# Expert outputs scattered to rows of their tokens, and w2 read in place by TensorE, in a retention and mixture-of-experts kernel

## The chip, the cores and the metric

The kernel runs on one core of a Trainium2 chip. The metric is the device time of one execution in microseconds (us), lower is better. Everything is float32.

## What is computed

Two sequences of 4096 tokens with 256 features each pass through one layer: a retention block with a gate, a layer norm, a mixture of eight experts of which each token uses two, and a second layer norm. Cut to what matters:

```python
q, v  = x @ Wq.T, x @ Wv.T                    # 16 heads of 16
state[t] = lam * state[t-1] + v[t]            # per channel, along the sequence
y     = layernorm(q * state) * ln_g + ln_b
x1    = layernorm(x + (y * silu(x @ Wg.T)) @ Wo.T)
gates = softmax(x1 @ gate_W)                  # 8 experts
cw    = the two largest gates, divided by their sum; 0 elsewhere
out   = x1
for e in range(8):
    h   = relu(x1 @ W1[e] + b1[e])            # 256 -> 512
    out = out + cw[:, e:e+1] * (h @ W2[e] + b2[e])   # 512 -> 256
out   = layernorm(out)
```

## The kernel before

**Tiles.** The 8192 tokens are 16 blocks of TB = 512, each held as 128 partitions x NT = 4 rows. `attention(i)` is a generator that does one block up to the routing; its `yield`s cut it into steps, which the main loop interleaves with steps of the neighbouring blocks and with expert work.

**Routing.** Each block's tokens find their two experts on VectorE (`largest`), and a matmul with a triangle of ones (lines 451 and 452) gives each token its row in its expert's region of a DRAM buffer `xs`. Eight indirect DMAs from GpSimd (line 470), one for each of 4 x 2 sets of 128 rows, scatter the rows of `x1` there. The blocks form two groups (`GROUPS = (13, 3)`: blocks 0 to 12 and 13 to 15), each with its own `xs` and `ys` buffers in DRAM. `plan_slots` turns the counts into slots: 256 rows of one expert where an expert has filled so many (SL = 256), and after the last block of a group slots of 128 rows for what is left, padded with zero rows that GpSimd writes (`put_zeros`, line 205). Group 0 has 45 slots of 256 and 21 of 128, group 1 has 5 and 21. Tiles and lines of the slots of 128 carry `_rest` in the profile.

**A slot.** `load_slot` reads the slot's row and expert number into SyncE registers and loads its 256 or 128 rows (`xg`) and the expert's w1 from DRAM. `slot_columns` transposes the rows on TensorE (line 590), VectorE copies them out (line 591), ScalarE reads the expert's number into a register (line 592) and copies that expert's w2, b2 and b1, 1284 floats per partition, from a table `kept` of all eight experts to a tile `wb` (line 596). `slot_first` is h (TensorE line 608, ScalarE's relu line 615), `slot_second` is h @ w2 (TensorE line 629, weights `hT`, moving operand `wb`) and VectorE's addition of b2 (line 633, output `ysl`, two buffers). `store_slot` writes the rows with a DMA from SyncE to `ys`, to the same rows as they had in `xs` (line 638); each store waits for the store before it.

**Combining.** When the last slot of a group is stored, `to_gather` gets all its blocks. `gather` takes 128 tokens: two indirect DMAs from GpSimd (line 654) read the tokens' two rows from `ys` by the row numbers `pos`, and at the first of a block SyncE loads the block's `x1` back (line 650, tile `sum`, three buffers). `weigh` adds the two rows with their weights on VectorE (line 669) and takes the statistics (lines 675 and 676), three gathers later (AHEAD = 3). `scale_of` makes the second norm's factor (a power on GpSimd, line 238), `end` applies it on ScalarE (line 689) and stores the block.

**Order.** TensorE, VectorE, ScalarE and SyncE run their instructions in the order in which the program lists them (`manual_schedule`). GpSimd isn't in that list, so the framework's scheduler orders its queue by itself. `half` does one half of a slot, and with it some combining of the group that is finished, paced by `debt`, so that group 0 is combined while group 1's slots run. Group 1 is combined after the last slot.

Of the kernel before, what the change touches and what calls it, by code (L numbers as in the profile page):

```python
# [15 lines left out]
P = 128  # L16
TB = 512
# [3 lines left out]
AHEAD = 3  # L21
# [10 lines left out]
def kernel(  # L32
# [22 lines left out]

    nc = tc.nc
# [18 lines left out]
    KEPT = NF * D + D + NF  # L75
# [5 lines left out]
    lam_sb = const.tile([P, NC, TB], FP, tag="lam", name="lam_sb")  # L81
# [43 lines left out]
    kept = const.tile([P, E, KEPT], FP, tag="kept", name="kept")  # L125

    def keep(e, after):
        at = 0
        for src, n in (
            (w2[e].rearrange("(c p) d -> p c d", p=P), NF),  # L130
            (b2[e : e + 1].partition_broadcast(P), 1),
            (b1[:, ts(e, NF)].unsqueeze(1), 1),
        ):
            size = n * src.shape[-1]
            dma = nc.sync.dma_start(
                out=kept[:, e, at : at + size].rearrange("p (c f) -> p c f", c=n), in_=src
            )
            at += size
            if after is not None:
                tc.add_manual_dep(dma.ins, after, SYNC, reason="not all at once")  # L140
                after = None
# [14 lines left out]
    m_rows = const.tile([1, MAXS, E], FP, tag="m_rows", name="m_rows")  # L156
    nc.vector.tensor_scalar_mul(m_rows, m_tab, float(SL))

    zeros = const.tile([P, D], FP, tag="zeros", name="zeros")
    nc.gpsimd.memset(zeros, 0.0)  # L160

    class Group:


        def __init__(self, k, n_blocks):
            self.k, self.n_blocks = k, n_blocks
            self.full = max(0, 4 * n_blocks - 7)
            self.rest = 8 * n_blocks + 7 - 2 * self.full
            assert self.rest <= MAXS
            self.cap = n_blocks * TB + P  # L170
            self.dump = E * self.cap
            rows = self.dump + (E - 1) * P
            self.xs = dram.tile([rows, D], FP, tag=f"xs_{k}", name=f"xs_{k}")
            self.ys = dram.tile([rows, D], FP, tag=f"ys_{k}", name=f"ys_{k}")

            self.first = const.tile([P, E], FP, tag=f"first_{k}", name=f"first_{k}")
            nc.gpsimd.iota(self.first, [[self.cap, E]], base=0, channel_multiplier=0,
                           allow_small_or_imprecise_dtypes=True)
            self.base = self.first
            self.taken = const.tile([1, E], FP, tag=f"taken_{k}", name=f"taken_{k}")  # L180
            nc.vector.memset(self.taken, 0.0)
            self.filled = []
            self.stored = []

            self.dumps = const.tile([1, MAXS, E], FP, tag=f"dumps_{k}", name=f"dumps_{k}")
            nc.vector.tensor_scalar(
                self.dumps, m_tab, float(E - 1 - self.rest), 0.0, ALU.add, ALU.max
            )
            nc.vector.tensor_scalar(
                self.dumps, self.dumps, float(P), float(self.dump), ALU.mult, ALU.add  # L190
            )
            self.off = const.tile([1, MAXS, E], FP, tag=f"off_{k}", name=f"off_{k}")
            nc.vector.scalar_tensor_tensor(
                self.off, m_tab, float(P), self.dumps, ALU.mult, ALU.subtract
            )
# [8 lines left out]
        def put_zeros(self, row):  # L204
            self.put(nc.gpsimd.dma_start(
                out=self.xs[ds(row, P), :], in_=zeros
            ))
# [7 lines left out]
        def store(self, dma):  # L215
            key = f"ys_{self.k}"

            tc.declare_no_dep(
                dma.ins, group=key, keep=self.stored[-1:], reason="rows of their own"
            )  # L220
            tc.add_to_no_dep_group(key, dma.ins)
            self.stored.append(dma.ins)

    groups = [Group(k, n) for k, n in enumerate(GROUPS)]
    for m in range(E - 1):
        for gr in groups:
            gr.put_zeros(gr.dump + m * P)
# [45 lines left out]
    def project(w, xT, o, name):  # L273
# [13 lines left out]
        dram.tile([P, NT, D], FP, tag=f"x1_{i}", name=f"x1d_{i}") for i in range(NB)  # L287
# [3 lines left out]
    def attention(i):  # L291
# [7 lines left out]
        for o in range(NC):  # L299
            v_ps = project(wv_sb, xT, o, f"v_{i}_{o}")  # L300
            first = i % BPS == 0
            nc.vector.tensor_tensor_scan(  # L302
                state[:, o, :],
                lam_sb[:, o, :],
                v_ps,
                0.0 if first else states[i - 1][:, o, TB - 1 : TB],
                ALU.mult,
                ALU.add,
            )
# [48 lines left out]
        rr = work.tile([P, NT, D], FP, tag="x1", name=f"x1_{i}", bufs=3)  # L358
        for t2 in range(NT // 2):
            o_ps = ps_a.tile([P, 2, D], FP, tag="pa", name=f"ao_{i}_{t2}")  # L360
            for u in range(2):
# [6 lines left out]
                rr[:, 2 * t2 : 2 * t2 + 2, :], o_ps, x_t[:, 2 * t2 : 2 * t2 + 2, :], ALU.add  # L368
# [3 lines left out]
        mv = row_stats(lambda t: rr[:, t, :], f"a{i}")  # L372
        r = rstd_of(mv[:, :, 1:2], f"a{i}")
        yield
        normalise(x1, lambda t: rr[:, t, :], mv, r, f"a{i}")
# [35 lines left out]
        def largest(src, name, hot):  # L411
# [9 lines left out]
            return top  # L421

        hot = small.tile([P, 2, NT, E], FP, tag="hot", name=f"hot_{i}")
        top1 = largest(g, "1", hot[:, 0])
# [3 lines left out]
        top2 = largest(rest, "2", hot[:, 1])  # L428
# [50 lines left out]
    def schedule(gr, j):  # L479
# [3 lines left out]
        if j == gr.n_blocks - 1:  # L483
# [3 lines left out]
            for e in range(E):  # L487
                gr.put_zeros(
                    nc.values_load(
                        ends[:, e : e + 1], engines=[ENG.Pool],  # L490
                        min_val=e * gr.cap, max_val=(e + 1) * gr.cap - P,
                    )
                )
            plan_slots(gr, f"{gr.k}_rest", gr.rest, True)

    def plan_slots(gr, name, n, rest):
# [52 lines left out]
        if rest:  # L549
            nc.vector.tensor_tensor(plan[:, 0, :n, :], at, gr.dumps[:, :n, 0:1], ALU.add)  # L550
        else:
            nc.vector.tensor_copy(plan[:, 0, :n, :], at)
# [7 lines left out]
    def load_slot(s):  # L560
# [8 lines left out]
        xg = slot.tile([P, SL // P, D], FP, tag="xg", name=f"xg_{name}", bufs=3)  # L569
# [13 lines left out]
    def slot_columns(s):  # L583
# [7 lines left out]
        nc.vector.tensor_copy(xgT, pt)  # L591
        e = nc.values_load(
# [4 lines left out]
        return gr, name, size, row, xgT, w1_t, wb[:, 0, :]  # L597

    def slot_first(s):
        gr, name, size, row, xgT, w1_t, wb = s  # L600
        b1_t = wb[:, NF * D + D :]
# [16 lines left out]
        return gr, name, size, row, hT, wb  # L618

    def slot_second(s):  # L620
        gr, name, size, row, hT, wb = s
        n_t = size // P
        w2_t = wb[:, : NF * D].rearrange("p (c d) -> p c d", c=NF)
        b2_t = wb[:, NF * D : NF * D + D].unsqueeze(1)
        y = slot.tile([P, SL // P, D], FP, tag="ysl", name=f"ysl_{name}")[:, :n_t, :]
        po = ps_s.tile([P, SL // P, D], FP, tag="ps", name=f"po_{name}")[:, :n_t, :]
        for t in range(n_t):
            for f in range(NF):
                nc.tensor.matmul(  # L629
                    po[:, t, :], hT[:, f, ts(t, P)], w2_t[:, f, :],  # L630
# [3 lines left out]
        return gr, size, row, y  # L634

    def store_slot(s):
        gr, size, row, y = s
        gr.store(nc.sync.dma_start(
            out=gr.ys[ds(row, size), :].rearrange("(p t) d -> p t d", p=P), in_=y
        ))  # L640
        left[gr.k] -= size // P
        if left[gr.k] == 0:
            to_gather.extend((i, t) for i in place if place[i][0] is gr for t in range(NT))

    def gather(i, t):

        gr, _ = place[i]
        if t == 0:
            sums[i] = work.tile([P, NT, D], FP, tag="sum", name=f"sum_{i}", bufs=3)
            nc.sync.dma_start(out=sums[i], in_=x1_dram[i])  # L650
        both = []
        for k in range(2):
            yk = work.tile([P, D], FP, tag=f"y{k}", name=f"y{k}_{i}_{t}", bufs=AHEAD + 2)
            dma = nc.gpsimd.indirect_dma_start(  # L654
                out=yk.bitcast(I32),
                out_offset=None,
                in_=gr.ys.bitcast(I32),
                in_offset=bass.IndirectOffsetOnAxis(ap=poss[i][:, k, t, :], axis=0),
            )
            for ins in gr.stored:  # L660
                tc.add_manual_dep(dma.ins, ins.name, SYNC, reason="rows stored before")
            both.append(yk)
        return i, t, both

    def weigh(i, t, both):

        x1, wt = sums[i], wts[i]
        for k, yk in enumerate(both):
            nc.vector.scalar_tensor_tensor(  # L669
                x1[:, t, :], yk, wt[:, k, t, :], x1[:, t, :], ALU.mult, ALU.add  # L670
# [4 lines left out]
        nc.vector.bn_stats(st, x1[:, t, :])  # L675
# [8 lines left out]
    def end(i):  # L684
# [3 lines left out]
        for t in range(NT):  # L688
            nc.scalar.activation(
                x1[:, t, :], x1[:, t, :], AF.Identity,  # L690
                bias=less[:, t, :], scale=r[:, t, :],
            )
        nc.scalar.dma_start(out=ob[i], in_=x1)

    loaded, turned, hidden, out_of = [], [], [], []
    to_gather, gathered, to_scale, to_end = [], [], [], []
# [13 lines left out]
    def combining():  # L710
        return to_gather or gathered or to_scale or to_end

    def some_combining(n):

        for _ in range(n):
# [4 lines left out]
            if to_gather:  # L720
                gathered.append(gather(*to_gather.pop(0)))
            if len(gathered) > AHEAD or (gathered and not to_gather):
                weigh(*gathered.pop(0))

    def half():
# [17 lines left out]
        debt[0] += len(to_gather) * size / (P * max(1, 2 * sum(left.values()) - 8))  # L743
# [14 lines left out]
    lam_col = const.tile([P, NC], FP, tag="lam_col", name="lam_col")  # L758
    nc.vector.tensor_copy(lam_col, lam_ps[:, :NC])
    for c in range(NC):  # L760
        nc.vector.tensor_copy(lam_sb[:, c, :], lam_col[:, c : c + 1].broadcast_to([P, TB]))
# [87 lines left out]
```

## Time and profile before

| | |
|---|---|
| median of 3 runs | 1097.53 us (1095.64 to 1101.23) |
| the profiled execution's own time | 1091.48 us |
| its span, first to last instruction | 1089.5 us |
| TensorE, VectorE, ScalarE, GpSimd busy | 899.7, 548.4, 386.1, 318.5 us |
| granted TensorE clock, mean | 0.924 |
| moved by DMA | 163.79 MB |

How to read it: PE is TensorE's matmuls, PEld its weight loads, DVE is VectorE, ACT ScalarE, POOL GpSimd, SP SyncE; a q behind an engine means its sequencer, which handles registers, waits and the issue of DMAs. A group of instructions is shown as line, engine, operation, output <- inputs, count, busy time in us and mean ns of one, then the engine's idle time before them and what ended it. In a table by stages each engine's column is its busy time in that stretch, with the number of instructions. "DMA share" is the mean busy share of the 16 DMA engines.

### The profile page before, as it was taken

Reading aid. Unit: us, or ns where it says so; the run is one execution under the profiler, and the core shown is the slowest. Engines: PE = TensorE matmul, PEld = TensorE weight load, DVE = VectorE, ACT = ScalarE, POOL = GpSimd, SP = SyncE. Lnnn points to the kernel's source line nnn. Section 1 sums busy time; section 2 is a strip of 40 time slices with the busy share of each in tenths; the row PEclk is TensorE's granted clock in tenths of the full one; section 3 lists DMA queues with packets and bytes.
Section 4 is the critical chain, followed back from the end, with each engine's and each line's share of the span. In section 5 each row is a group of like instructions: output and inputs, shape, how many; then the busy total and the mean of one; then the engine's idle time right before and its main releaser. Section 6 shows DMA issues by size and latency. Waiting matters only on the chain. (4 is left out here: it accounts for less than half of the span.)

```text
span 1089.5 us, 14838 instructions
## 1 busy us (share of the span) xinstructions
PE 899.7 (83%) x4366; PEld 713.7 (66%) x4366; DVE 548.4 (50%) x1841; ACT 386.1 (35%) x733; POOL 318.5 (29%) x346
## 2 busy tenths in 40 slices
PE   4988586899899999999999999999898965776710
PEld 2555354778677777778786868688797854666610
DVE  2675544356455554555455455534334245665544
ACT  1221212323333334343333323334454423554412
POOL 3112321302030303030211203130304367676454
PEclk9998796999999999999999999999899988888965
DMA  5611214232333424242434342443647857988653
GB/s 192 205 54 44 88 60 143 99 124 88 133 119 126 151 101 161 94 151 88 146 102 131 112 131 97 164 155 128 193 155 226 269 182 246 281 296 267 229 175 110
DMA packets 95041, 163.79 MB, mean 150 GB/s; under 512 B 12081, under 2 KB 45361, under 8 KB 94961
## 3 DMA queue, kind: packets, MB, share of 16 engines
q1 hardware_dynamic: 68800, 107.52, 30.6%
q0 software_dynamic: 13728, 37.50, 10.4%
q10 hardware_dynamic: 12432, 17.84, 4.5%
q8 instruction: 34, 0.56, 0.2%
q14 instruction: 47, 0.38, 0.1%
HBM read 106.72 MB, written 56.10 MB: 149 GB/s over the span
## 5 line engine op out<-in xcount | busy, mean ns | idle before, releaser
L629 PE MATMUL po<-wb,hT 128*128 128x256 f32 x800 | 190.3, 393 | 8.1 <-issue 6.2
L608 PE MATMUL ph<-xgT,w 128*128 128x256 f32 x800 | 185.8, 386 | 10.4 <-DVE xgT L591 10.4
L608 PEld LDWEIGHTS ph<-xgT,w 128*128 128x128 f32 x800 | 154.1, 194 | 36.9 <-DVE xgT L591 11.2
L629 PEld LDWEIGHTS po<-wb,hT 128*128 128x128 f32 x800 | 153.6, 197 | 29.7 <-issue 7.1
L470 POOL DMA_INDIRECT xs<-x,pos x128 | 124.4, 972 | 142.8 <-DVE rows L512 102.1
L615 ACT ACTIVATE hT<-ph,wb 128x256 f32<-128x256 f32 x200 | 83.9, 471 | 211.3 <-PE ph L608 149.8
L654 POOL DMA_INDIRECT y<-ys,pos x128 | 125.5, 981 | 81.3 <-issue 29.9
L238 POOL TENSOR_TENSOR rstd_a<-rstd_a,half_neg 128x4 f32<-128x4 f32 x16 | 16.1, 1007 | 429.5 <-DVE rstd_a L237 429.5
L629 PE MATMUL po_rest<-wb_rest,hT_rest 128*128 128x256 f32 x336 | 89.6, 415 | 18.0 <-DVE rstd_f L237 12.8
L608 PE MATMUL ph_rest<-xgT_rest,w_rest 128*128 128x128 f32 x672 | 89.3, 290 | 18.2 <-DVE xgT_rest L591 12.4
L591 DVE COPY xgT<-xt 128x512 f32<-128x512 f32 x50 | 34.5, 691 | 137.1 <-PE xt L590 110.1
L608 PEld LDWEIGHTS ph_rest<-xgT_rest,w_rest 128*128 128x128 f32 x672 | 86.9, 204 | 24.1 <-DVE xgT_rest L591 14.2
L615 ACT ACTIVATE hT_rest<-ph_rest,wb_rest 128x128 f32<-128x128 f32 x168 | 48.1, 369 | 116.3 <-PE ph_rest L608 45.8
L629 PEld LDWEIGHTS po_rest<-wb_rest,hT_rest 128*128 128x128 f32 x336 | 67.0, 210 | 29.1 <-issue 16.3
L633 DVE TENSOR_TENSOR ysl<-po,wb 128x512 f32<-128x512 f32 x50 | 34.3, 686 | 85.9 <-PE po L629 33.5
L276 PE MATMUL g<-xT,wg_sb 128*128 128x512 f32 x128 | 61.4, 621 | 8.4 <-DVE state L302 5.0
L596 ACT COPY wb<-kept 128x1284 f32 x50 | 63.1, 1262 | 3.8 <-DVE ysl L633 0.9
L669 DVE SCALAR_TENSOR_TENSOR sum<-y,wt,sum 128x256 f32<-128x256 f32 x128 | 61.5, 481 | 5.5 <-DMA y<-ys,pos 3.3
L276 PE MATMUL q<-xT,wq_sb 128*128 128x512 f32 x128 | 59.7, 610 | 0.4 <-ACT yg L351 0.4
L276 PE MATMUL v<-xT,wv_sb 128*128 128x512 f32 x128 | 59.5, 609 | 0.3 <-issue 0.3
L363 PE MATMUL ao<-wo_sb,yg 128*128 128x256 f32 x256 | 58.2, 380 | 0.9 <-DVE y L326 0.9
L596 ACT COPY wb_rest<-kept 128x1284 f32 x42 | 53.5, 1275 | 5.0 <-DVE ysl_rest L633 3.6
(143 smaller groups left out, 1097.9 us busy)
## 6 DMA issues: line engine op xcount, KB each, us to landing
w<-in_w_dram SPq DMA_DIRECT2D x50, 512.0 KB
w_rest<-in_w_dram SPq DMA_DIRECT2D x42, 512.0 KB
xg<-xs SPq DMA_DIRECT2D x50, 256.0 KB
ys<-ysl SPq DMA_DIRECT2D x50, 256.0 KB
x<-in_x_dram SPq DMA_DIRECT2D x16, 512.0 KB
x1d<-x ACTq DMA_DIRECT2D x16, 512.0 KB
sum<-x1d SPq DMA_DIRECT2D x16, 512.0 KB
out_dram<-sum ACTq DMA_DIRECT2D x16, 512.0 KB
```

Of the source, the lines that this page charges most:

```text
L238: nc.gpsimd.tensor_tensor(r, r, half_neg[:, :n, :], ALU.pow)
L276: last = nc.tensor.matmul(ps, w[:, c, ts(o, P)], xT[:, c, :], start=(c == 0), stop=(c == NC - 1))
L363: nc.tensor.matmul(o_ps[:, u, :], yg[:, c, ts(2 * t2 + u, P)], wo_sb[:, c, :], start=(c == 0), stop=(c == NC - 1),)
L470: gr.put(nc.gpsimd.indirect_dma_start(out=gr.xs, out_offset=bass.IndirectOffsetOnAxis(ap=pos[:, k, t, :], axis=0), in_=x1s[i][:, t, :], in ...
L591: nc.vector.tensor_copy(xgT, pt)
L596: nc.scalar.copy(wb, kept[:, ds(e, 1), :])
L608: nc.tensor.matmul(ph[:, u, :], w1_t[:, c, ts(f0 + u, P)], xgT[:, c, :], start=(c == 0), stop=(c == NC - 1),)
L615: nc.scalar.activation(hT[:, f, :], ph[:, u, :], AF.Relu, bias=b1_t[:, f : f + 1])
L629: nc.tensor.matmul(po[:, t, :], hT[:, f, ts(t, P)], w2_t[:, f, :], start=(f == 0), stop=(f == NF - 1),)
L633: nc.vector.tensor_tensor(y, po, b2_t.broadcast_to([P, n_t, D]), ALU.add)
L654: dma = nc.gpsimd.indirect_dma_start(out=yk.bitcast(I32), out_offset=None, in_=gr.ys.bitcast(I32), in_offset=bass.IndirectOffsetOnAxis(ap= ...
L669: nc.vector.scalar_tensor_tensor(x1[:, t, :], yk, wt[:, k, t, :], x1[:, t, :], ALU.mult, ALU.add)
```

## The change

Rows in `xs` get eight more floats (ROW = 264): the first carries the number of the token's pair of output rows (2 x the token's number in its group), the second the rank of the token's first expert. `ys` is laid out by tokens: two rows for each token, one for each of its experts, so that a block's outputs are 1 MB in one piece. A slot keeps the two numbers of its rows (`whose`), and VectorE makes from them the rows to write: the pair's number, plus one where this slot's expert is the token's first (`to`). `store_slot` becomes one indirect DMA from GpSimd for each 128 rows; the stores no longer wait for each other. `gather` is gone: `load_sum` loads a block's `x1` and its 1 MB of `ys` with two plain DMAs from SyncE, the second of which waits for all the group's scatters; `weigh` takes its rows from that tile (`y2`, two buffers). Padding rows carry row numbers behind all tokens. Pacing counts loads as well as weighings. Besides, w2 of all experts stays in a table of its own, `w2_sb`, and the second matmul of a slot reads it there at a place that a TensorE register gives; `wb` holds b2, b1 and the expert's rank only (261 floats per partition). The retention scan takes its decay from one column, broadcast, instead of a filled tile.

```diff
-    KEPT = NF * D + D + NF
+    ROW = D + 8
+    KEPT = D + NF + 1
...
+    def put_none(rows, k, n):
+        rows = rows.rearrange("(n p) d -> p n d", p=P)
+        return (
+            nc.gpsimd.dma_start(out=rows[:, :, :D], in_=zeros.broadcast_to([P, n, D])),
+            nc.gpsimd.dma_start(out=rows[:, :, D:], in_=none[:, k : k + n, :]),
+        )
+
+    no_rows = dram.tile([E * P, ROW], FP, tag="no_rows", name="no_rows")
+    put_none(no_rows, 0, E)
...
-    for m in range(E - 1):
-        for gr in groups:
-            gr.put_zeros(gr.dump + m * P)
+    for gr in groups:
+        for dma in put_none(gr.xs[gr.dump :, :], E, E - 1):
+            gr.put(dma)
...
-                lam_sb[:, o, :],
+                lam_col[:, o : o + 1].broadcast_to([P, TB]),
...
+        nc.vector.tensor_scalar_add(rr[:, :, D:], number, float(2 * TB * place[i][1]))
...
+        nc.vector.tensor_copy(x1[:, :, D + 1 : D + 2], first)
...
+        whose = slot.tile([P, SL // P, 2], FP, tag="whose", name=f"whose_{name}", bufs=4)
+        whose = whose[:, : size // P, :]
+        nc.vector.tensor_copy(whose, xg[:, : size // P, D : D + 2])
...
     def slot_second(s):
-        w2_t = wb[:, : NF * D].rearrange("p (c d) -> p c d", c=NF)
+        e = nc.values_load(plan[0:1, 1, m, :], engines=[ENG.PE], min_val=0, max_val=E - 1)
...
-                    po[:, t, :], hT[:, f, ts(t, P)], w2_t[:, f, :],
+                    po[:, t, :], hT[:, f, ts(t, P)], w2_sb[:, ds(e, 1), f, :],
...
+        to = slot.tile([P, SL // P, 1], I32, tag="to", name=f"to_{name}")[:, :n_t, :]
+        nc.vector.scalar_tensor_tensor(
+            to, whose[:, :, 1:2], wb[:, KEPT - 1 :], whose[:, :, 0:1], ALU.is_equal, ALU.add
+        )
...
     def store_slot(s):
-        gr.store(nc.sync.dma_start(
-            out=gr.ys[ds(row, size), :].rearrange("(p t) d -> p t d", p=P), in_=y
-        ))
+        for t in range(size // P):
+            gr.store(nc.gpsimd.indirect_dma_start(
+                out=gr.ys,
+                out_offset=bass.IndirectOffsetOnAxis(ap=to[:, t, :], axis=0),
+                in_=y[:, t, :],
+                in_offset=None,
+            ))
...
+    def load_sum(i):
+        gr, j = place[i]
+        x1 = work.tile([P, NT, ROW], FP, tag="sum", name=f"sum_{i}", bufs=3)
+        nc.sync.dma_start(out=x1, in_=x1_dram[i])
+        y2 = work.tile([P, NT, 2, D], FP, tag="y2", name=f"y2_{i}")
+        dma = nc.sync.dma_start(
+            out=y2,
+            in_=gr.ys[ts(j, 2 * TB), :].rearrange("(t p k) d -> p t k d", t=NT, p=P),
+        )
+        for name in gr.stored:
+            tc.add_manual_dep(dma.ins, name, SYNC, reason="rows stored before")
+        sums[i] = x1
+        to_weigh.extend((i, t, y2) for t in range(NT))
...
-            if to_gather:
-                gathered.append(gather(*to_gather.pop(0)))
-            if len(gathered) > AHEAD or (gathered and not to_gather):
-                weigh(*gathered.pop(0))
+            if to_load and len(to_weigh) <= NT:
+                load_sum(to_load.pop(0))
+            elif to_weigh:
+                weigh(*to_weigh.pop(0))
...
-        debt[0] += len(to_gather) * size / (P * max(1, 2 * sum(left.values()) - 8))
+        todo = 5 * len(to_load) + len(to_weigh)
+        debt[0] += todo * size / (P * max(1, 2 * sum(left.values()) - 8))
```

## The prediction

> **What bounds the kernel now.** I cut the run at two moments: the first gather of group 0 (857.8 us) and the end of TensorE's last matmul (1039.6). The table by stages:
>
> ```profile
> core 0: us, PE busy (x) PEld busy (x) DVE busy (x) ACT busy (x) POOL busy (x), PEclk, DMA share, GB/s
> 0.00:857.80 857.80, 770.94 (x3682) 602.71 (x3683) 427.20 (x1503) 295.59 (x547) 175.71 (x202) 0.96 0.39 129
> 857.80:1039.60 181.80, 128.80 (x686) 111.01 (x684) 96.90 (x269) 80.14 (x166) 115.16 (x116) 0.87 0.76 249
> 1039.60:1089.50 49.90, 0.00 (x0) 0.00 (x0) 24.34 (x70) 10.37 (x20) 27.64 (x28) 0.55 0.48 150
> ```
>
> Stage 1 is TensorE's (90% busy; 96% from 300 to 657 us) with GpSimd at 20%. In stage 2 group 1's slots run beside group 0's combining: TensorE is 71% busy at a lower clock, GpSimd 63%, the DMA engines 76%. Stage 3 has no matmul. The page's groups tell what GpSimd does:
>
> ```profile
> L629 PE MATMUL po<-wb,hT 128*128 128x256 f32 x800 | 190.3, 393 | 8.1 <-issue 6.2
> L470 POOL DMA_INDIRECT xs<-x,pos x128 | 124.4, 972 | 142.8 <-DVE rows L512 102.1
> L654 POOL DMA_INDIRECT y<-ys,pos x128 | 125.5, 981 | 81.3 <-issue 29.9
> L596 ACT COPY wb<-kept 128x1284 f32 x50 | 63.1, 1262 | 3.8 <-DVE ysl L633 0.9
> ```
>
> A gather costs 0.96 us and the next starts 0.30 later ("issue" in the timeline), so a block of 8 costs GpSimd 10.1 us, 11.4 with its rstd. The x1 loads of stage 2, one a block, start every 13.3 us ((1020.5 - 861.4)/12, from the records of their packets). GpSimd's gathers set this pace; VectorE, in order, waits for them, and with it the copies that TensorE needs. The timeline of the end:
>
> ```profile
> 1039.59 0.42 DVE L633 TENSOR_TENSOR ysl_rest<-po_rest,wb_rest 128x256 f32<-128x256 f32 x1 [1.30 <-PE po_rest L629]
> ...
> 1042.79 1.01 POOL L654 DMA_INDIRECT y<-ys,pos  x1 [12.96 <-DMA ys<-ysl_rest]
> ...
> 1066.40 1.04 POOL L238 TENSOR_TENSOR rstd_f<-rstd_f,half_neg 128x4 f32<-128x4 f32 x1
> 1067.48 0.16 DVE L687 SCALAR_TENSOR_TENSOR less<-mvf,rstd_f 128x4 f32<-128x4 f32 x1 [7.82 <-POOL rstd_f L238]
> ...
> 1084.90 0.38 ACTq L693 DMA_DIRECT2D out_dram<-sum  x1
> ```
>
> 24 gathers and the rstds behind them fill GpSimd from 1042.79 to 1075; VectorE waits 7.8 us for one rstd. So stage 3, and largely stage 2, is bound by GpSimd's gathers.
>
> [...] TensorE's sequencer made its check before line 590 at 407.62 us, and the weight load behind that check starts at 411.27. The lead is 3.4 to 4.0 us in stage 1 while slots are full, about 2.0 with slots of 128. [...] Stage 2's records show the clock at 0.5 in pieces of 3.4 to 10.2 us; mean 0.87. [...] here a 512 KB x1 load takes 2.2 to 3.0 us from first to last packet, so I take 5 us for 1 MB.
>
> **The change part by part**, against the profiled execution (span 1089.5, own time 1091.5; the median is 6.0 above that).
>
> *Start.* The 14 zero fills (0.54 us each on GpSimd) become 6 DMAs over 2,816 rows in two pieces each. At 0.54 per 128 pieces that is 24 us of GpSimd from 3 us on; its next work, the first rstd_y, starts at 32.7. Hidden. The DMA engines get 1,024 more KB (2,816 instead of 1,792 rows); at the 275 GB/s of 27 to 41 us that is 3.8 us if all on the path. Bounds 0 to 4, I take **+1.5**. The end-of-group fills stay as many (8 a group), and lie outside the path.
>
> *Register read on TensorE.* No TensorE register read is in this trace. ScalarE does the same read of the same plan for line 596:
>
> ```profile
> L592 ACTq FUSED_REGOPS  x92: 152/152/173, 128.6 to 1032.9; - x92
> L592 ACTq SEQ_ASSERT  x92: 18/18/33, 128.8 to 1033.1; - x92
> L592 ACTq TENSOR_LOAD <-plan x50: 273/284/812, 128.1 to 884.6; - x50
> ```
>
> With 0.046 for each address (line 596), 0.28 + 0.15 + 0.02 + 0.05 = 0.50 us a slot, 0.82 if all 8 matmuls make their own. Ahead of it in TensorE's queue wait 16 pairs of weight load and matmul (2 us or more). ScalarE[...] hides it: the copy at 400.74 follows the relu before it without a gap, and line 596 waited 3.8 us in 50. So the lead covers it, but for a few slots before 857 us where it is short: **0**. With the lead gone it is 92 x 0.50 = 46 us, up to 75. A gain from it alone I exclude: the same matmuls read as many bytes.
>
> *w2 copies go.* ScalarE's 92 copies fall from 1.26 to about 0.47 us (line 615's 128x256): 73 us less on an engine that is 34% busy in stage 1 and 44% in stage 2. Other engines waited for these copies for some 14 us in all, TensorE for 2 of them. Bounds -5 to 0, I take **0**; next late is line 608's result for the relu, as now.
>
> *Scatters instead of stores.* SyncE loses 92 stores of 0.36 us and their waits (the store's line waited 127 us for ysl). Queued behind them were loads of xg and w1, but TensorE waited only 9 us for xg in the whole run: 0. GpSimd gets 142 scatters of 1.26 us pitch; group 0's 111 make 140 us on top of 175.7 in stage 1: 37% busy. Behind a scatter that waits for `ysl` queue rstd_y, rstd_a and the scatters of line 470; VectorE waits for the rstds. In the steady block of 451 to 502 us the ysl additions are at 459.4, 467.6, 476.4, 497.4, rstd_a at 458.3, the eight scatters at 464.9 to 474.8, rstd_y at 479.6. Only the scatters of the third meet an rstd (rstd_y), for up to 1.5 us; VectorE's scan keeps it 1.1 us away anyhow, and the transposes behind (line 350, 488.5) have 5 us to spare. **0**; if each of 32 rstds lost 2.5 us, +80 on VectorE, some +28 after the slack.
>
> *Small VectorE work.* `whose` and `to`, about 0.16 each (the row `less_a` shows 0.154), are 0.32 x 92 = 29 us, beside an engine at 50%: hidden behind TensorE. The two additions per block, 0.36 us, lie in the routing chain; TensorE has slack except while few slots are there (100 to 300 us, 75 to 90% busy): 5 blocks x 0.36, **+2**. The broadcast scan: same elements at 1.27 us, 0 (bounds -2 to +2).
>
> *Stage 2.* GpSimd loses 104 gathers and gains 31 scatters: 131 us less 39. The next limit is the DMA engines: 0.765 x 181.8 = 139 us of work, the same bytes (rows in another order, +3% on x1 and xg, +1 us), then TensorE, 129. SyncE gets a wait: the second load of a block for the scatters once, and for the buffer of two blocks earlier, so for VectorE; xg and w1 of later slots queue behind, but three slots are loaded ahead. At a DMA share of 0.85, between the 0.76 of now and the 0.94 of the page's best slice, 140/0.85 = 165: **-17** (bounds 0 and -33).
>
> *Stage 3.* From 1039.6: addition and `to` 0.6, scatter 1.0, landing 2 (a gather's row was used 1.3 us after its issue), issue and first packet 1.4, 1 MB 5.0: 1049.6. Each block is weighed in 4 x 1.57 = 6.3 us ((2 x 0.48) + 0.43 + 0.18): 1055.9 and 1062.2; the third's load waits for the first's buffer, 1055.9 + 6.4 = 1062.3, so 1068.6. rstd 1.4, less and ScalarE 2.3, store and end 4.6 as now: 1076.9, **-12.6** (bounds -17 and -6).
>
> Sum: 1.5 + 0 + 0 + 0 + 2 - 17 - 12.6 = -26 us: own time 1065, **median 1071.5**.
>
> **Rivals.** *A: stage 2 stays as long.* For it: the DMA share is already 0.76, and in 900 to 1000 us it is 0.84. Against: 104 gathers leave the engine that sets the pace. Time 1097.5 - 26 + 17 = 1088.5; a gain still. *B: GpSimd's queue order costs as much as it brings,* rstds behind waiting scatters, +28: 1099.5. For it: that queue is ordered by the scheduler's estimate, and at the end of this run one rstd stood behind five gathers. Against: the free 80% of stage 1. *C, slower: TensorE's sequencer stops at the register read.* Place: ahead of each line 629. Price 0.50 us x 92 = 46: 1097.5 - 26 + 46 = 1117.5 (75: 1146). It decides from 26/92 = 0.28 us exposed per slot. For it: no such read is in the trace, and the lead is shortest where slots of 128 follow each other (0.0 to 1.6 us at 831 to 853). Against: the leads above.
>
> **How the numbers follow.** Forecast 0.47 (1050 to 1084), A 0.14 (1080 to 1092), B 0.13 (1090 to 1105), C 0.26 (1105 to 1146). About 0.5% is what a measurement of this kernel can tell from no change: below 1092 faster, above 1103 slower. Faster: forecast, A and a little of B, 0.62; same: most of B, 0.11; slower: C and a rest of B, 0.27. The range reaches from both gains at their bounds (1097.5 - 33 - 17 + 3, about 1050) to C's price with its 0.50, 1118, leaving out some 0.17 above and 0.02 below. Likeliest alone: 1050 to 1084.
>
> **What would show it.** Right: stage 1 as long as before within 6 us, line 629 with no new "issue" idle, stage 2 near 165 us with a DMA share over 0.8, the end after the last matmul near 37 us. Wrong: idle of 0.3 to 0.8 us before each line 629 (C), VectorE's `less_y` and `less_a` waiting for GpSimd (B), stage 2 at 180 us with SyncE waiting for line 669 (A).

## The result, and the profile after

The kernel after takes 1125.87 us (median of 4 runs, 1122.17 to 1129.48), the kernel before beside it 1096.59 (1093.73 to 1101.23): ratio 1.0263, 95% interval 1.0213 to 1.0313. It is slower by 29 us; 26 us less were predicted. The profiled execution took 1125.09 us, its span 34.0 more than that of before.

One thing must be known for all that follows: the runs fell on several chips. On some, this one among them, the kernel before takes 1090 to 1097 us, on others 1057 to 1062. So each experiment is compared with the kernel before on its own chip, and the two kinds of chip turn out to tell the causes apart.

The table by stages of the kernel after, cut as in the prediction: at the first load of expert outputs (928.2 us) and at the end of the last matmul.

```profile
core 0: us, PE busy (x) PEld busy (x) DVE busy (x) ACT busy (x) POOL busy (x), PEclk, DMA share, GB/s
0.00:928.20 928.20, 802.87 (x3692) 622.98 (x3693) 444.40 (x1677) 237.77 (x550) 281.42 (x308) 0.93 0.38 123
928.20:1081.90 153.70, 119.36 (x675) 101.79 (x674) 104.47 (x328) 60.87 (x167) 42.11 (x42) 0.94 0.87 297
1081.90:1123.50 41.60, 0.00 (x0) 0.00 (x0) 19.56 (x58) 8.29 (x16) 5.35 (x6) 0.56 0.47 159
```

Stage 2 fell from 181.8 to 153.7 us and stage 3 from 49.9 to 41.6; both were to fall, by 17 and 12.6. Stage 1, which was to grow by 3.5 us, went from 857.8 to 928.2. (Before's first gather is at 860.4 us in its timeline, 2.6 later than the prediction cut. With that cut its three stages are 860.4, 179.2 and 49.9, and the differences used below are +67.8, -25.5 and -8.3.) The groups on the page show the moved work:

```profile
L656 PE MATMUL po<-w_sb,hT 128*128 x800 | 195.5, 401 | 11.3 <-issue 5.3
L671 POOL DMA_INDIRECT ys<-ysl,to x100 | 98.1, 981 | 319.5 <-DVE to L663 242.0
L495 POOL DMA_INDIRECT xs<-x,pos x128 | 123.2, 963 | 62.4 <-issue 27.1
```

The scatters cost what was assumed, and line 656 (629 before) waits for "issue" 5.3 us in 800 matmuls, no more than the 6.2 of before. The loss is in the waits of a block. The timeline of one block's end in the kernel after (start, length, engine and line; in brackets the idle time before, and its releaser):

```profile
548.77 0.96 POOL L495 DMA_INDIRECT xs<-x,pos  x1 [2.10 <-DVE rows L536]
...
554.31 0.60 PE L614 MATMUL xt<-ident,xg 128*128 128x128 f32 x4
554.74 3.62 PE L656 MATMUL po<-w_sb,hT 128*128 x16
...
560.14 0.96 POOL L671 DMA_INDIRECT ys<-ysl,to  x1 [0.30 <-issue]
560.94 0.69 DVE L615 COPY xgT<-xt 128x512 f32<-128x512 f32 x1 [8.64 <-PE v L299]
...
563.05 0.64 PE L293 MATMUL pt_x<-ident,x 128*128 128x128 f32 x4 [0.38 <-issue]
563.28 0.69 DVE L660 TENSOR_TENSOR ysl<-po,wb 128x512 f32<-128x512 f32 x1 [1.57 <-issue]
...
566.36 2.44 DVE L325 TENSOR_TENSOR_SCAN state<-lam_col,state,v 128x512 f32<-128x512 f32 x2
...
567.69 0.69 PE L293 MATMUL pt_x<-ident,x 128*128 128x128 f32 x4 [3.99 <-DVE state L325]
568.18 5.30 PE L635 MATMUL ph<-xgT,w 128*128 128x256 f32 x16
...
580.52 5.39 PE L656 MATMUL po<-w_sb,hT 128*128 x16
```

The same place in the kernel before:

```profile
473.81 0.96 POOL L470 DMA_INDIRECT xs<-x,pos  x1 [0.31 <-issue]
...
476.38 0.69 DVE L633 TENSOR_TENSOR ysl<-po,wb 128x512 f32<-128x512 f32 x1 [4.58 <-PE yt L336]
...
480.67 0.66 PE L270 MATMUL pt_x<-ident,x 128*128 128x128 f32 x4 [1.39 <-DVE state L302]
481.16 3.62 PE L608 MATMUL ph<-xgT,w 128*128 128x256 f32 x16
...
491.81 3.70 PE L629 MATMUL po<-wb,hT 128*128 128x256 f32 x16
```

From 548.77 to 561.1 GpSimd issues ten scatters in a row, eight of x1 and two of a slot whose `ysl` came meanwhile; before it is eight. TensorE's transposes `xt` end at 554.9, but VectorE's copy of them starts at 560.94; `po` ends at 558.4, and the addition starts at 563.28. Behind it, VectorE's scan is late, TensorE waits 3.99 us for it instead of 1.39, its clock falls to half twice, and `ph` takes 5.30 instead of 3.62, `po` 5.39 instead of 3.70. That is 2.60 + 1.68 + 1.69 = 6.0 us a block. From scan to scan a block takes 57.35 us between 336 and 680 us, 51.2 before: 6.15. (On the clock: its record in the trace shows 0.5 for 3.4 us from 568.2, behind the wait of 3.99 us, and once more for 3.4 us from 581.8, where the longest idle time since is 0.48 us. What makes it fall was not shown.)

What holds VectorE back? The trace also records when semaphores change; the releasers in the brackets are inferred from this. The changes that TensorE's matmuls make, its completion signals, normally follow the end of the matmul by 0.01 us (578 of the 645 on record come within 0.15 us, the median of these is 0.014). In this stretch that of `xt` comes at 560.92, that of `po` at 563.20, and the four behind it at 563.26 to 563.43: one bunch, 2.1 us after the last scatter's issue ended. In the kernel before three signals come in such a bunch at 476.3, 1.5 us after the last of eight scatters. The ends of matmuls are modelled in the profile, and what stands between an end and its signal was not shown. Here the gap is up to 6.0 us. The matmuls themselves were not late by as much: in their rows TensorE works without a pause from 550.9 us to the end of `v` at 562.7, rests 0.38 us, and `pt_x` behind it, which ends at 563.70, has its signal on time again.

### The profile page after: what moved, and what is told of

It is laid out like the page before. It is cut to its first block, busy times and chain, and to the rows that moved or that the text cites. A ratio compares the mean times of both kernels' runs of the same rounds, so it can differ in the third digit from the quotient of the medians.

```text
span 1123.5 us, 15516 instructions
## 1 busy us (share of the span) xinstructions
PE 922.2 (82%) x4366; PEld 724.8 (65%) x4366; DVE 568.4 (51%) x2063; ACT 306.9 (27%) x733; POOL 328.9 (29%) x355
## 4 chain that ended last, share of the span: by engine, by line
PE 60%; DVE 14%; issue 8%; DMA 7%; POOL 6%; ACT 2%; another core or an unknown queue 1%; POOLq 0%; SPq 0%; DVEq 0%; ACTq 0%
PE po L656 14%; PE ph L635 14%; PE q L299 5%; PE ao L387 5%; PE g L299 4%; PE po_rest L656 3%; DVE sum L700 3%; POOL xs L495 3%; PE lg L411 3%; PE ph_rest L635 3%; PE v L299 3%; DMA xg_rest<-xs 2%; PE pt_x L293 2%; PE xt L614 2%; DVE bnst_f L707 1%
## 5 line engine op out<-in xcount | busy, mean ns | idle before, releaser
L635 PE MATMUL ph<-xgT,w 128*128 128x256 f32 x800 | 199.6, 407 | 14.0 <-DVE xgT L615 10.4
L656 PE MATMUL po<-w_sb,hT 128*128 x800 | 195.5, 401 | 11.3 <-issue 5.3
L635 PEld LDWEIGHTS ph<-xgT,w 128*128 128x128 f32 x800 | 164.2, 207 | 45.0 <-DVE xgT L615 11.2
L671 POOL DMA_INDIRECT ys<-ysl,to x100 | 98.1, 981 | 319.5 <-DVE to L663 242.0
L656 PEld LDWEIGHTS po<-w_sb,hT 128*128 128x128 f32 x800 | 157.1, 201 | 34.8 <-issue 5.6
L656 PE MATMUL po_rest<-w_sb,hT_rest 128*128 x336 | 89.7, 415 | 22.4 <-issue 11.6
L656 PEld LDWEIGHTS po_rest<-w_sb,hT_rest 128*128 128x128 f32 x336 | 65.9, 206 | 35.0 <-issue 12.9
L671 POOL DMA_INDIRECT ys<-ysl_rest,to_rest x42 | 41.2, 981 | 142.2 <-DVE to_rest L663 95.1
L261 POOL TENSOR_TENSOR rstd_a<-rstd_a,half_neg 128x4 f32<-128x4 f32 x16 | 16.5, 1033 | 187.0 <-DVE rstd_a L260 187.0
L293 PE MATMUL pt_x<-ident,x 128*128 128x128 f32 x256 | 39.2, 291 | 35.7 <-DVE state L325 26.7
L700 DVE SCALAR_TENSOR_TENSOR sum<-y,wt,sum 128x256 f32<-128x256 f32 x128 | 61.2, 478 | 13.4 <-DMA y<-ys 11.1
L293 PEld LDWEIGHTS pt_x<-ident,x 128*128 128x128 f32 x256 | 31.3, 148 | 51.0 <-DVE state L325 28.8
```

The costliest lines, as they stand in the source:

```text
L293: nc.tensor.transpose(pt[:, ts(t, P)], src[:, t, ts(c, P)], ident)
L635: nc.tensor.matmul(ph[:, u, :], w1_t[:, c, ts(f0 + u, P)], xgT[:, c, :], start=(c == 0), stop=(c == NC - 1),)
L656: nc.tensor.matmul(po[:, t, :], hT[:, f, ts(t, P)], w2_sb[:, ds(e, 1), f, :], start=(f == 0), stop=(f == NF - 1),)
L671: gr.store(nc.gpsimd.indirect_dma_start(out=gr.ys, out_offset=bass.IndirectOffsetOnAxis(ap=to[:, t, :], axis=0), in_=y[:, t, :], in_offset ...
L700: nc.vector.scalar_tensor_tensor(x1[:, t, :D], y2[:, t, 1 - k, :], wt[:, k, t, :], x1[:, t, :D], ALU.mult, ALU.add,)
```

## The experiments

Three theories: **register theory** (the prediction's rival C), **queue theory** (rival B: rstds or buffers behind scatters), **held-signal theory** (a long row of scatters holds TensorE's signals back; VectorE, in order, passes the delay on).

**First group** (kernel before 1091.23 us, signals late as above). *e1*: `bufs=4` for `ysl` and `to`. 

> The kernel after, with four buffers instead of two for ysl and to. In the kernel after, VectorE's addition of the last slot of a block begins 5 us after the matmuls it needs, and TensorE then waits 4.0 us for the scan behind it (57.6 us a block instead of 51.2). Buffer theory: the addition waits until the scatter of two slots earlier, queued behind the eight scatters of x1, has landed; then it falls to some 51 us a block and 1055 to 1070 us. Scatter theory and register theory: the buffers are free in time; 1120 to 1130 us, still 57 to 58 us a block.

Measured 1119.53, ratio 1.0255 (1.0206 to 1.0303), 57.3 us a block. Not the buffers, apart from some 6 us after the last block's scan, to which I return. *e2*: the kernel before, with

```diff
+        e = nc.values_load(plan[0:1, 1, m, :], engines=[ENG.PE], min_val=0, max_val=E - 1)
-                    po[:, t, :], hT[:, f, ts(t, P)], w2_t[:, f, :],
+                    po[:, t, :], hT[:, f, ts(t, P)], w2_sb[:, ds(e, 1), f, :],
```

> The kernel before, with w2 in a table of its own that TensorE reads through a register, wb with biases only; stores and gathers as before. Register theory (the read on TensorE's queue holds back the engines that wait for TensorE): the stage up to the first gather gets 6 us a block longer, 1150 to 1170 us. Scatter theory: no loss, 1090 to 1100 us, 51.2 us a block, line 629's counterpart with no more issue idle than now.

Measured 1092.17, ratio 1.0007 (0.9994 to 1.0019), 51.2 us a block: the register and the copies gone, taken together, change nothing. *e3*: the kernel after, with w2 copied per slot to `wb` as before. 

> The kernel after, with w2 copied for each slot by ScalarE as in the kernel before and no register on TensorE; scatters and plain loads as in the kernel after. Scatter theory (GpSimd's longer queue carries the loss): 1118 to 1135 us, 57 to 58 us a block. Register theory: 1055 to 1070 us, 51 us a block. If both carry a part: between, 1080 to 1110.

Measured 1121.68, ratio 1.0257 (1.0216 to 1.0297), 57.3 us a block. The whole loss goes with the scatters and what came with them, not with w2.

**Second and third group** (kernel before 1057.10 and 1057.98: the other kind of chip). *e7*: the kernel before with, behind the eight scatters,

```diff
+        for k in range(2):
+            spare = nc.gpsimd.indirect_dma_start(
+                out=more, out_offset=bass.IndirectOffsetOnAxis(ap=pos[:, k, NT - 1, :], axis=0),
+                in_=x1s[i][:, NT - 1, :], in_offset=None)
```

> The kernel before, with two more scatters of 128 rows of x1 behind the eight of each block, to a DRAM buffer that nothing reads; all else as before. Held-signal theory (while GpSimd issues a long row of scatters, TensorE's completion signals reach the other engines late, and come only when the last scatter has landed): ten in a row cost what they cost in the kernel after, 57 to 58 us a block instead of 51.2, and 1145 to 1175 us. Queue theory (the loss is work of GpSimd, the rstds, that stands behind scatters): rstd_y becomes ready 2 us after the ten, so no loss; 1089 to 1098 us.

Measured 1071.82, ratio 1.0140 (1.0087 to 1.0192), 51.3 us a block; 1071.40 in the third group. Neither theory's number. But in none of these eight traces does one of TensorE's some 700 signals come more than 0.15 us late, in that of the kernel before (*b0*, 1062.03 us) neither. So what I had taken for a property of the kernel belongs to the chip as well. *a0*, the kernel after itself, there: 

> The kernel after, unchanged, beside the kernel before on the same chip. Held-signal theory: where signals come late, ratio 1.02 to 1.03 and 57 to 58 us a block; where they do not, about 51.3 us a block and a ratio of 0.98 to 1.0. Queue theory: ratio 1.02 to 1.03 on either chip, 56 to 58 us a block.

Measured 1070.72 in two runs, ratio 1.0125 (1.0031 to 1.0218), 51.0 us a block. The loss of 6 us a block is gone, though twelve scatters stand in a row here; and still the kernel is slower. The stages of b0 and then of a0:

```profile
0.00:854.20 854.20, 782.79 (x3690) 612.17 (x3691) 430.07 (x1504) 295.83 (x550) 175.47 (x203) 0.95 0.39 131
854.20:1010.20 156.00, 121.23 (x677) 105.52 (x675) 95.80 (x267) 78.68 (x164) 114.48 (x116) 0.92 0.86 285
1010.20:1060.40 50.20, 0.03 (x1) 0.00 (x0) 24.34 (x70) 10.37 (x20) 27.50 (x28) 0.54 0.48 152
```

```profile
0.00:871.70 871.70, 785.82 (x3689) 613.44 (x3690) 445.08 (x1677) 237.98 (x550) 281.30 (x308) 0.94 0.39 131
871.70:1029.90 158.20, 124.44 (x679) 104.92 (x677) 104.58 (x328) 60.97 (x167) 42.17 (x42) 0.91 0.85 290
1029.90:1071.40 41.50, 0.00 (x0) 0.00 (x0) 19.57 (x58) 8.30 (x16) 5.34 (x6) 0.56 0.46 159
```

Stage 1 loses 17.5 us, in three places (times of the scans): 3.8 at the first, 4.9 more by 330 us (1.6 are won back), 10.4 after the last block's scan, where the trace shows VectorE waiting twice, 12.3 us in all, for scatters behind the last rows to give a buffer of `ysl` back:

```profile
DVE ysl_rest L660 <- DMA ys<-ysl_rest,to_rest: 12.3, 2, 7.2
```

Stage 2 is as long as before (158.2 and 156.0, DMA share 0.85 and 0.86), with 72 us less work on GpSimd: here stage 2 stays as long, as rival A had it. Three more kernels of these groups missed their mark. *e8*: scatters two slots later, so that none should follow the eight; a slot's later addition came early enough that twelve stood in a row, as in a0. 

> The kernel after, with the scatters of a slot issued two slots later (they wait for the addition of the second next slot; five buffers for ysl and to), so that the eight scatters of x1 have none directly behind them. Held-signal theory: as in the kernel before, 51 to 52.5 us a block, 1050 to 1072 us. Queue theory (rstd_y still stands behind scatters that wait): 57 us a block, 1115 to 1135 us.

Measured 1058.78, ratio 1.0010 (0.9985 to 1.0034); again, 1058.97. *e6*, before, and *e5*, after, make GpSimd wait inside the row:

```diff
+                if 2 * t + k and (2 * t + k) % 4 == 0:
+                    landed = nc.gpsimd.memset(pause, 0.0)
+                    tc.add_manual_dep(landed.ins, gr.filled[-1], SYNC, reason="in parts")
```

> The kernel before, with the eight scatters of a block in two parts: the fifth to eighth wait on GpSimd until the fourth has landed (a memset of 128 floats between them carries the wait). Held-signal theory: no signal is held for long, VectorE's addition follows TensorE at once, TensorE's wait of 1.4 us a block for the scan goes; 49.5 to 50.5 us a block, 1070 to 1082 us. Queue theory: a row longer by 1.5 us changes nothing; 1089 to 1096 us.

> The kernel after, with the eight scatters of a block in parts of three, three and two: each part waits on GpSimd until the part before has landed; the scatters of the slots stand between as the scheduler places them. Held-signal theory, if a pause of some 1.5 us sets the signals free: 51 to 53 us a block, 1055 to 1085 us; if a pause is too short for it: 56 to 58 us, 1115 to 1130 us. Queue theory: GpSimd's row gets longer, so the loss grows, 1125 to 1145 us.

e6: 1066.50, ratio 1.0076 (1.0051 to 1.0101), and 1.0087 (1.0051 to 1.0122) in the fifth group. e5: 1089.33, ratio 1.0305 (1.0253 to 1.0358). Where no signal is late there is nothing to set free. I read the cost as that of slots waiting longer for their rows; that is argued, not isolated. Nor was either kernel run where signals are late.

**Fourth group** (kernel before 1091.25, signals late again). *e7c* is e7. 

> The kernel before with ten scatters a block instead of eight, once more. Held-signal theory: on a chip where TensorE's completion signals come late (kernel before at 1090 to 1098 us) 57 to 58 us a block and 60 to 80 us over the kernel before; on one where they do not (1057 us), 12 to 15 us over as before. Queue theory: 12 to 15 us over on either chip.

Measured 1147.92, ratio 1.0513 (1.0468 to 1.0559): 57 us over the kernel before, where the same kernel loses 15 on the other chips. A block takes 55.9 us; both are a little under what was expected. Its timeline has no scatter of expert outputs, and yet the same waits as the kernel after:

```profile
541.34 1.03 POOL L471 DMA_INDIRECT xs<-x,pos  x1 [5.59 <-DVE rows L522]
...
552.81 0.97 POOL L478 DMA_INDIRECT more<-x,pos  x1 [0.30 <-issue]
555.13 0.60 PE L271 MATMUL pt_x<-ident,x 128*128 128x128 f32 x4
555.67 0.69 DVE L643 TENSOR_TENSOR ysl<-po,wb 128x512 f32<-128x512 f32 x1 [7.41 <-PE v L277]
...
558.87 1.04 POOL L239 TENSOR_TENSOR rstd_y<-rstd_y,half_neg 128x4 f32<-128x4 f32 x1 [5.09 <-DVE rstd_y L238]
559.96 1.07 PE L271 MATMUL pt_x<-ident,x 128*128 128x128 f32 x4 [4.22 <-DVE state L303]
```

TensorE waits 4.22 us for the scan (3.99 in the kernel after), and rstd_y finds GpSimd idle: it is not work behind the row in GpSimd's queue, but the row. *e10*: the kernel after with the six fills made to wait for the second block's last projection, and `bufs=5` for `ysl` and `to`. 

> The kernel after with two edits: the six fills wait for the last projection of the second block instead of standing at the start, and ysl and to have five buffers. Fill and buffer theory: the start gets 3.8 us shorter, the stage from 690 us to the first y load some 8 us; on a chip without late signals 1055 to 1060 us beside 1070 of the kernel after, on one with late signals 1108 to 1116 beside 1120 to 1126. If neither is a cause: as the kernel after, 1066 to 1074 or 1118 to 1128.

Measured 1110.64, ratio 1.0178 (1.0137 to 1.0219), 57.3 us a block: 11 us below e3 and 9 below e1 (which ran on another chip of this kind), the first scan at 16.8 instead of 24.1 us. *e11*: e10 with the row in halves. 

> The kernel of e10 with the eight scatters of a block in two parts, the second waiting on GpSimd until the first has landed. Held-signal theory: on a chip with late signals some 51 to 54 us a block, 1070 to 1100 us, below e10; on one without, 5 to 15 us over e10, because slots wait longer for their rows. Queue theory: over e10 on either chip.

Measured 1106.41, ratio 1.0133 (1.0106 to 1.0161), but 57.0 us a block: the scheduler put a slot's scatters into the pause, and ten stand in a row as before (541.4 to 553.9 us). It tells nothing on a broken row. *e9*: e8 with the fills of e10. 

> The kernel with scatters two slots later (as e8) and with the fills of e10. On a chip without late signals: 3 to 4 us under e8, 1054 to 1057 us, 0.995 to 1.0 of the kernel before. On a chip with late signals the row of scatters is no shorter (twelve, since the later ones queue directly behind), so held-signal theory: 57 us a block and 1105 to 1120 us; queue theory: as on the other chip, 0.995 to 1.0 of the kernel before.

Measured 1111.02, ratio 1.0194 (1.0159 to 1.0229), 57.3 us a block, rows of ten: as held-signal theory expected.

**Fifth and sixth group** (kernel before 1059.62 and 1061.20, no late signals). *e12*: e10, and no scatter of a slot between the eight and the second addition behind them:

```diff
-        elif out_of:
-            store_slot(out_of.pop(0))
+        elif out_of and (quiet[0] <= 0 or not (hidden or turned or loaded or slots)):
+            late = len(out_of) > 1
+            while out_of:
+                store_slot(out_of.pop(0), late)
```

(`quiet` is set to 2 behind the eight, and each addition takes one off; late scatters wait for the latest addition.) 

> The kernel of e10 (fills later, five buffers), and after the eight scatters of a block no slot's scatter is issued before the second addition behind them; the two slots then waiting are scattered together. Held-signal theory: rows stay at eight, so on a chip with late signals 51 to 52.5 us a block and 1062 to 1080 us beside 1091 of the kernel before; on a chip without, 51.3 us a block and 1052 to 1062 us, within 5 us of the kernel before. Queue theory (rstd_y stands behind four scatters now): slower than e10 on either chip, over 1110 or over 1062 us.

Measured 1051.24, ratio 0.9922 (0.9894 to 0.9949), and once more 1050.93, ratio 0.9922 (0.9891 to 0.9952): by 0.8% the one kernel that beats the one before. Its stages:

```profile
0.00:850.10 850.10, 781.69 (x3689) 610.48 (x3690) 444.89 (x1677) 236.54 (x550) 281.43 (x308) 0.95 0.41 134
850.10:1009.30 159.20, 123.31 (x679) 104.49 (x677) 105.06 (x329) 60.86 (x167) 41.24 (x41) 0.92 0.85 288
1009.30:1051.80 42.50, 0.00 (x0) 0.00 (x0) 19.55 (x58) 8.29 (x16) 6.16 (x6) 0.56 0.47 155
```

All 17.5 us of stage 1 are back against b0, and stage 3 keeps its gain. (Stage 1 is 4 us shorter than in b0, but b0 ran 4 us above the median on its own chip.) Rows are of eight in all blocks but the one at 772 us, where thirteen stand together. Both times it met a chip without late signals, so whether it also saves the 6 us a block where they come late was not seen.

The times of a full block, scan to scan, between 320 and 680 us:

| scatters in a row | chips with late signals | chips without |
|---|---|---|
| 8 | 51.2 (before), 51.2 (e2) | 51.3 (b0), 51.3 (e12) |
| 10 | 57.35 (after), 57.3 (e1, e3, e9, e10), 55.9 (e7c) | 51.3 (e7) |
| 12 | not run | 51.0 (a0), 51.1 (e8) |

That a row of eight seems to cost nothing in the left column is partly luck. In b0's full blocks TensorE never waits for the scan, where the kernel before waits 1.39 us a block. But b0's `po` behind `lg` meets one half-speed window a block, with no idle time over 0.48 us ahead of it, and the kernel before meets none between 290 and 754 us:

```profile
489.26 1.95 PE L387 MATMUL lg<-gw_sb,x1T 128*128 128x8 f32 x16 [0.48 <-ACT yg L351]
491.07 5.39 PE L629 MATMUL po<-wb,hT 128*128 128x256 f32 x16
```

So of the 6.0 us above, the 1.69 of `po` is not shown to come from late signals. Against a0, which has that window too and no wait, the wait of 3.99 and the 1.68 of `ph` make 5.7 of 6.3 us a block.

## Why the prediction was wrong

**Scatters instead of stores, 0: the step that failed.** It looked at whom the scatters delay in GpSimd's queue, and found the third slot's harmless. That was right (`less_y` and `less_a` wait 16.5 and 4.7 us for GpSimd in the whole run, 18.4 and 4.6 before). But the row of eight became ten, and on this kind of chip the row acts on another engine: TensorE's signals come late behind it, and TensorE's wait for the scan grew from 1.39 to 3.99 us a block. The sign was in the trace of before, an addition 1.9 us after its matmuls and that wait of 1.39 us; I read it as VectorE's own order. The bound of +28 was made for waiting rstds, and was too small too: stage 1 lost 67.8 us against 17.5 where no signal is late, so by this difference between chips some 50 us come from late signals. Two scatters alone cost 57 - 15 = 42 of that kind in e7.

**Start, +1.5** (0 to 4): 4.0, the first scan at 24.1 instead of 20.1 us. Mechanism right (the fills' traffic, ahead of a small load, `lng_sb`, for which VectorE waits 14.6 us instead of 12.0), size at its bound; e10 takes it back.

**Buffers of `ysl`**: not in the sum. At the end of group 0, where scatters stand behind rows and fills, VectorE waits for a buffer; e1 gives 6 us of the 12 back that stage 1 loses there (181.7 us from the last block's scan to the first load, 188.1 in the kernel after, 176.0 before).

**Register read, 0, and copies gone, 0**: right for the two together, by e2. The read is there, as long as ScalarE's, and hidden:

```profile
L651 PEldq FUSED_REGOPS  x92: 151/151/165, 142.1 to 1077.7; - x92
...
L651 PEldq TENSOR_LOAD <-plan x50: 296/301/489, 141.5 to 962.6; - x50
L651 PEldq TENSOR_LOAD <-plan_rest x42: 297/302/1208, 807.2 to 1077.3; - x42
```

So rival C, which brought the prediction's slower end, fell too.

**Stage 2, -17** (0 to -33): -25.5 here, within its bounds, but not for the reason given; +2 and +3 on the other chips (a0 and e12 against b0). GpSimd's gathers were to be what sets the pace. In b0 they do follow nearly back to back, a block's eight every 11.1 us against the 11.4 that they and the rstd cost, and yet the stage is no shorter without them: in a0 the loads of `ys` start every 10.9 us, at a DMA share of 0.85 after 0.86. That the DMA engines are the limit there fits these shares; no run isolates it. In the kernel before on this chip a block's gathers start every 12.7 us, so GpSimd had time to spare; the same instructions take 179.2 us there and 156.0 in b0, and there TensorE's signals come late behind gathers as well (37 of the 89 on record in stage 2 by over 0.15 us). That late signals are the whole difference of 23 us is likely, not isolated.

**Stage 3, -12.6** (-17 to -6): -8.3. The third block's factor is asked for 30.5 us after the last matmul, 29.0 in the working. The missing rest is the last store, 7.5 us to the end instead of 4.6:

```profile
1081.93 0.42 DVE L660 TENSOR_TENSOR ysl_rest<-po_rest,wb_rest 128x256 f32<-128x256 f32 x1 [1.12 <-PE po_rest L656]
...
1112.36 0.17 DVE L260 TENSOR_SCALAR rstd_f<-mvf 128x4 f32<-128x4 f32 x1
...
1116.04 0.38 ACTq L725 DMA_DIRECT2D out_dram<-sum  x1
```

**Small VectorE work, +2**: not seen apart; e12, which has it, has a stage 1 shorter than before.

**Rivals.** B, "GpSimd's queue order", named the right part and nearly the right place, but by another mechanism and with 28 us where some 50 are lost. None of the rivals let one engine's queue delay the signals of another.

## What to carry to other kernels

When work moves to an engine with spare time, ask what it lengthens, not only what it fills: a row of eight scatters became ten, and where signals come late, blocks became 12% longer on an engine that issues none of them. Where an instruction in a trace starts well after its input's end and the named releaser is a later instruction of the producer ("xgT waits for v"), look up when the signal came. And compare kernels on one chip: the same pair of kernels came to a ratio of 1.0263 on one and 1.0125 on another, for different reasons.

## What the hardware showed

On the chips with the kernel before at 1091 to 1097 us, some 50 to 90 of TensorE's signals in a run came more than 0.15 us after the matmul's end (79 of 669 on record in the kernel before, 65 of 645 in the kernel after; the count isn't exact, since some records are missing), mostly in bunches 1 to 2.4 us after the last scatter of a row of eight or more had been issued, with single ones set free inside the row, and in stage 2 also around shorter rows. On the chips with 1057 to 1061 us not one did, behind rows of up to twelve scatters or eighteen gathers; in e12 VectorE's addition at the end of a row of eight starts 0.09 us after its matmuls (472.63 us). Signals of VectorE, ScalarE and GpSimd that are on record came in time in the kernels before and after (3922 of 3935 within 0.15 us of an instruction's end, the median 0.01), and GpSimd's own pace (0.96 us and 0.30) is the same on both kinds. On the first kind of chip the trace also lacks records of some signals (of TensorE's 710 in the kernel before it has 669, of VectorE's 1604 it has 1390; on the second kind TensorE's are all there). Late signals and lost records thus come together, and no run here shows whether signals would be late without the recording: that the recording itself holds them back is a rival that stands untested. Why the signals are held, and what sets the chips apart, stays open too.
